# A float32 fast-matrix-product kernel: a changed model for its instruction order, bank halves in the end products, and two subtractions on another engine

## The chip, the cores and the metric

The kernel runs on one core of a Trainium2 chip. A core has four compute engines that the profile names PE (TensorE, the matrix unit; its weight loads are listed apart as PEld), DVE (VectorE), ACT (ScalarE) and POOL (GpSimd). SP (SyncE) only issues transfers. Engines have instruction queues of their own and wait for each other through semaphores. TensorE writes into PSUM, an accumulator memory in eight banks, which VectorE and ScalarE read; all else lies in SBUF. The metric is device time in microseconds (us): the median of several executions of the whole kernel.

## The reference

With 1024 rows of `x`, 512 features `f`, 512 outputs `m` and 64 embeddings `e`:

```python
out_lin = x @ lin_w.T + lin_b
xv = jnp.einsum('bf,efm->bem', x, weight)
zp = jnp.einsum('bf,efm->bem', jnp.square(x), jnp.square(weight))
interaction = 0.5 * jnp.sum(jnp.square(xv) - zp, axis=1)
return out_lin + interaction
```

The sum over `e` of `zp` needs no big product: it is the product of the squares of `x` with the sum over `e` of the squares of `weight`, of the size of the linear part. The big work is `xv`, whose squares are summed over `e`.

## The kernel before

**Work.** The product `xv` is cut into 22 groups of output columns, two of 16 and then twenty of 24 columns, each times 64 embeddings. A group's quarters of the weight arrive by DMA. Sums and differences of the quarters are made, partly by GpSimd transfers that add into SBUF (`dma_add`, lines 462 to 466, called by `outer_sum` and `outer_out`). Seven products (`ORDER`) replace the eight of a two-by-two block product. Each is a *tree*: `tree` (line 729) replaces eight smaller products by seven, with matmuls 384 columns wide in the large groups; `wide_tree` (line 818) has 20 matmuls 256 wide, and takes products 1, 5 and 7 of the large groups. Weight-side sums (`t`) are made by GpSimd. Partial results stay in PSUM banks and are copied from bank to bank by ScalarE (`copy`, line 435) or taken out by VectorE with an addend (`tt`, line 421). At the end ScalarE squares the results and VectorE sums them over `e` into `acc`.

**PSUM.** There are four pairs of banks: `b1`, `b3`, `b2_0`, `b2_1`. A pair is one tensor, and there is also one tensor for each bank of it (`b_l`, `b_r` in the profile), which `wide_tree` uses. The planner keeps its dependencies by banks (its atoms have the size of one bank).

**Small products.** `outer_products` (line 587) does one two-by-two block product with seven `big` products (line 521), each of eight matmuls 256 wide over a whole pair of banks. It is called twice: at the start by `lin` for the linear part, and at the end for the squares' product. In it one pair is copied to another two times, `copy(pair(u2), pair("b1"))` at line 591 and `copy(pair(u3), pair(u2))` at line 599. `big` takes a list of parts `(k, j0, j1)`; as a rule the parts are `(0, 0, 4)` and `(1, 0, 4)`: first weight half 0 over all four cells (both banks), then half 1. The last product alone, at line 603, has four parts that finish the left bank first. Its closing function `leave(0, 1, u2)` reads the pair in two halves at the end of the kernel.

**The end.** While the last trees still run, VectorE adds the summed squares to the linear part in `add_acc` (the instructions at L1043), and the left sides of the squares' product, `xs[3]`, `xs[5]`, `xs[6]`, `xs[7]`, are made of squared blocks of `x`. A `tt` without PSUM operands goes to GpSimd; `minus_both` (line 573; its instruction is L576 in the profile) is one VectorE instruction that gives minus a minus b.

**The order of the work.** All operations are first entered in a `Plan`. `Plan.order` (line 183) then runs its own model of the engines, with a cost for each operation, a fixed `HOP` between an operation's end and its reader's start, a slower rate where VectorE and GpSimd are both at work in SBUF, and one queue for adding transfers. Each engine takes among the ready operations the one with the earliest `latest`, a due time worked out backwards from TensorE's fixed sequence of matmuls and then shifted by an offset from the table `AHEAD_OF` (eighths of a microsecond in base 36, one entry for each position in a part of the program; all even groups share one part, all odd groups another). TensorE takes the ready operation with the lowest key. The order in which the model starts operations is the order in which the program is emitted; each engine's queue is therefore fixed when the kernel is built.

Of the kernel before, what the change touches and what calls it, by code (L numbers as in the profile page):

```python
# [41 lines left out]
0:-1d 1:28mt 2:1rdw 3:28qb 4:28sp 5:1rhs 6:1r1z 7:1o2z 8:r13 9:1ny7 a:3m5 b:1qhi c:1nqc d:1okx e:1qxc f:m62  # L42
g:m61 h:3it i:3jq j:16r0 k:t l:4 m:-k n:v o:2m p:1v q:2s r:1 s:-1 t:o u:-e v:14 w:n x:i y:4 z:k 10:e 11:203
12:1d 13:-1e 14:-8 15:12 16:29 17:v 18:c 19:1m 1a:g 1b:-1g 1c:-5 1d:-2 1e:4oo 1f:-i 1g:-9 1h:k 1i:8 1j:18
1k:-1a 1l:1 1m:-k 1n:19 1o:9 1p:-5 1q:1m 1r:-q 1s:b 1t:-o 1u:1o 1v:4 1w:1d 1x:-1d 1y:-5 1z:j 20:2 21:-1 22:h
23:-j 24:-g 25:3 26:-6 27:w 28:-b 29:-f 2a:x 2b:b 2c:-t 2e:31 2f:-5 2g:1 2h:-a 2i:-7 2j:-u 2k:j 2l:1 2m:r
2n:-v 2o:x 2p:9 2q:3 2r:e 2s:r 2t:-b 2u:-5 2v:p 2w:5 2x:a 2y:a 2z:-l 30:-1 31:-n 32:-3 33:-e 34:i 35:2h 36:s
37:-g 38:-f 39:12 3a:8 3b:z 3c:y 3d:-f 3e:7 3f:-k 3g:h 3h:o 3i:-o 3j:cp 3k:14 3l:1d 3m:x 3n:n 3o:5 3p:-3 3q:-k
3r:k 3s:e 3t:-5 3u:-u 3v:dc 3w:-7 3x:-14 3y:9 3z:23 40:7 41:7 42:c 43:-2 44:-19 45:q 46:-f 47:-3 48:-5 49:-4
4a:-8 4b:-1a 4c:j 4d:-q 4e:2a 4f:3 4g:-3 4h:d 4i:b 4j:s 4k:g 4l:5 4m:6 4n:-16 4o:-c 4p:7 4q:4 4r:-i 4s:q 4t:-b  # L50
4u:-1t 4v:-11 4w:1v 4x:-4 4y:e1 4z:-f 50:-m4 51:-h 52:m 53:p 54:-c 55:12 56:-5 57:-p 58:a 59:-14 5a:-1 5b:-a
5c:-14 5d:-q 5e:-10 5f:-j 5g:-1a 5h:c 5i:2j 5j:g 5k:-18 5l:-1v 5m:fa 5n:-1 5o:k 5p:p 5q:-h 5r:1a 5s:-1r 5t:16
5u:1p 5v:3 5w:q 5x:m 5y:-5 5z:-h 60:r 61:w 62:9 63:-6 64:-1 65:m 66:s 67:x 68:o 69:-2 6a:-17 6b:d 6c:z 6d:-e
6e:-u 6f:-19 6g:f 6h:e 6i:-j 6j:-6 6k:-16 6l:-8 6m:7 6n:-7 6o:-23 6p:-l 6q:-25 6r:t 6s:1z 6t:u 6u:-k 6v:-1
6w:8 6x:-h 6y:2 6z:-14 70:-9 71:-t 72:13 73:1l 74:12 75:h 76:-2p 77:-g 78:i 79:a 7a:-6 7b:16 7c:19 7d:19 7e:r
7f:1b 7g:17 7h:-w 7i:-j 7j:-28 7k:-1m 7l:f 7m:16 7n:9 7o:-w 7p:l 7q:c 7r:-j 7s:-m 7t:2a 7u:5 7v:-k 7w:-5 7x:7
7y:-e 7z:1j 80:9 81:3 82:-8 83:-13 84:-21 85:-1h 86:16 87:-7 88:-14 89:-6 8a:-b 8b:-1e 8c:-1s 8d:2l 8e:o 8f:-7
8g:-t 8h:-e 8i:10 8j:14 8k:r 8l:d 8m:-m 8n:5 8o:-v 8p:18 8q:-g 8r:-v 8s:-6 8t:12 8u:w 8v:12 8w:1y 8x:1n 8y:b
8z:b 90:5 91:18 92:-19 93:-8 94:-h 95:7 96:5 97:f7 98:w 9a:19 9b:-u 9c:-a 9d:9 9e:-b 9f:6 9g:p 9h:-n 9i:-9
9j:6 9k:18 9l:-8 9m:-1 9n:1m 9o:1w 9p:14 9q:11 9r:t 9s:g 9t:-p 9u:u 9v:5 9w:-3 9x:-m 9y:-16 9z:-n a0:-q a1:25  # L60
a2:1k a3:-1l a4:1j a5:7 a6:-2 a7:-1l a8:11 a9:-n aa:dg ab:t ac:-1f ad:-1 ae:-8 af:l ag:-1f ah:1n ai:-6 aj:15
ak:2k al:6 am:y an:3 ao:-1m ap:b aq:-z ar:2 as:p at:3 au:-1 av:-1 aw:-1t ax:g ay:26 az:-t b0:9e b1:u b2:7
b3:-1t b4:-k b5:31 b6:-1p b7:18 b8:t b9:1c ba:8 bb:1y bc:-1n bd:-w be:-3 bf:15 bg:q bh:n bi:-j bj:-6 bk:g bl:i
bm:h bn:8 bo:2 bp:6 bq:-d br:21 bs:-x bt:a bu:-4 bv:1 bw:-t bx:-2 by:-d bz:j c0:-10 c1:-q c2:1d c3:-g c4:-16
c5:22 c6:-1k c7:-2n c8:-15 c9:d ca:-1k cb:6 cc:7 cd:r ce:-t cf:7 cg:-m ch:i ci:-t cj:5 ck:-2d cl:-o cm:-13
cn:-k co:-k cp:p cq:d cr:27 cs:-t ct:-v cu:-1 cv:-1 cw:6 cx:-7 cy:a cz:-3 d0:-1k d1:-1 d2:d d3:9 d4:-s d5:u
d6:16 d7:-4 d8:f d9:-18 da:1a db:-19 dc:-2t dd:-d de:k df:12 dg:c dh:-1y di:-1a dj:3 dk:q dl:-12 dm:-7 dn:-r
do:g dp:-11 dq:-i dr:19 ds:-2g dt:z du:-2e dv:g dw:-e dx:14 dy:v dz:-3z e0:x e1:17 e2:-d e3:-6 e4:l e5:-7
e6:-d e7:n e8:-22 e9:-t ea:5 eb:-q ec:10 ed:l ee:3 ef:9 eg:a eh:1a ei:f ej:-p ek:-v el:3 em:-s en:1s eo:23
ep:6 eq:-28 er:s es:c et:z eu:13 ev:-u ew:5 ex:-1q ey:s ez:-i f0:-7 f1:q f2:-a f3:l f4:-u f5:l f6:f f7:3 f8:d  # L70
f9:-t fa:17 fb:1 fc:-u fd:-i fe:-2 ff:-a fg:j fh:2 fi:-b fj:-2 fk:i fl:1e fm:g fn:-4 fo:1j fp:r fq:-s fr:-16
fs:-27 ft:7 fu:-1c fv:-3 fw:1s fx:i fy:i fz:a g0:4 g1:-15 g2:u g3:-2q g4:32 g5:6 g6:-3c g7:-s g8:-1 g9:-1c
ga:j gb:-2 gc:-1g gd:-2 ge:-s gf:-u gg:1g gh:1i gi:-6 gj:-1e gk:-6 gl:x gm:-i gn:r go:-u gp:-i gq:9 gr:-a gs:3
gt:-b gu:-7 gv:15 gw:-d gx:-1 gy:29 gz:-6 h0:-z h1:1d h2:v h3:-3 h4:7 h5:-j h6:1x h7:-e h8:-6 h9:-u ha:7 hb:2
hc:-w hd:c he:-3 hf:d hg:h hh:-10 hi:19 hj:-b hk:14 hl:-j hm:-5 hn:-1a ho:t hp:b hq:-18 hr:-s hs:-2x ht:-n
hu:b hv:-y hw:-w hx:-1 hy:-1x hz:1d i0:r i1:1 i2:-p i3:-z i5:c i6:1t i7:-s i8:-13 i9:1r ia:-j ib:-6 ic:-2r
id:2 ie:n if:3 ig:p ih:1l ii:l ij:1e ik:5 il:a im:-11 in:-1k io:6 ip:-o iq:-1w ir:17 is:16 it:8 iu:y iv:-11
iw:-b ix:-d iy:x iz:1p j0:-b j1:-c j2:l j4:-7 j5:-c j6:-e j7:8 j8:l j9:b ja:a jb:1 jc:m jd:-h je:p jf:-h jg:-3
jh:-j ji:7 jj:7 jk:2 jl:t jm:-c jn:-a jo:1l jp:-2 jq:m jr:-i js:y jt:-r ju:-l jv:-k jw:18 jx:-r jy:-2 jz:n
k0:11 k1:1q k2:-j k3:-h k4:a k5:-g k6:7 k7:8 k8:1 k9:3 ka:b kb:-3 kc:-a kd:-2 ke:-f kf:-y kg:-n kh:-11 ki:-6  # L80
kj:8 kk:-4 kl:-1a km:z kn:6 ko:-4 kp:f kq:-8 kr:-6 ks:-u kt:-1h ku:-gc kv:-18 kw:-m kx:-16 ky:1 kz:-3o l0:-2b
l1:-1o l2:-1f l3:q l4:e l5:v l6:-1e l7:-27 l8:-14 l9:10 la:h lb:-9 lc:16 ld:o le:2 lf:-n lg:-5 lh:d li:-i
lj:-f lk:-a ll:z lm:10 ln:-v lo:4 lp:6 lq:17 lr:1j ls:-q lt:-1b lu:k lv:h lw:-1c lx:6 ly:t lz:-n m0:-1p m1:1x
m2:-1b m3:-16 m4:-1 m5:1c m6:-z m7:-21 m8:-9 m9:-1w ma:y mb:-1r mc:-p md:-3 me:e mf:-c mg:c mh:1 mi:-5 mj:w
mk:14 ml:o mm:-9 mn:7 mo:-2 mp:-1 mq:-11 mr:-j ms:s mt:-2 mu:-r mv:45 mw:-11 mx:-1b my:-1a mz:q n0:r n1:i
# [12 lines left out]
tb:1t tc:n td:7 te:-3 tf:-u tg:7 th:1j ti:-1m tj:3 tk:-x tl:19 tm:-t tn:e to:-k tp:-a tq:s tr:-2b tt:-6 tu:-5
tv:o tw:1b tx:s ty:j tz:i u0:a u1:1e u2:-u u3:i u4:-6 u5:-j u6:8 u7:2 u8:9 u9:-q ua:1d ub:-1 uc:-r ud:2 ue:-8
uf:-2l ug:-1 uh:w ui:-6 uj:22 uk:-p ul:5 um:-r un:1t uo:-1h up:-5 uq:-8 ur:-7 us:-1b ut:-1a uu:-7 uv:p uw:8  # L100
ux:-a uy:14 uz:18 v0:-m v1:r v2:-20 v3:-o v4:-c v5:-9 v6:-1g v7:10 v8:-2g v9:t va:1d vc:-4 vd:16 ve:-24 vf:-1g
vg:18 vh:-2 vi:-18 vj:-2 vk:-5 vl:-h vm:-3 vn:-s vo:v vp:s vq:d vr:j vs:3 vt:n vu:8 vv:-g vw:d vx:-2y vy:v
vz:s w0:7 w1:-r w2:-2g w3:-2b w4:-17 w5:-12 w6:h w7:f w8:-r w9:-13 wa:-10 wb:-10 wc:-12 wd:k we:-g wf:-4 wg:h
# [32 lines left out]
AHEAD = 20.0  # L136
# [3 lines left out]

def groups(n_m):
    return [16, 16] + [24] * ((n_m - 32) // 24)


class Plan:
    HOP = 0.18

    def __init__(self):
        self.ops = []
        self.writer = {}  # L150
        self.readers = defaultdict(list)
        self.signs = {}
# [30 lines left out]
    def order(self, spare=SPARE):  # L183
# [9 lines left out]
        t = 0.0  # L193
# [953 lines left out]
```

## Time and profile before

| what | us |
|---|---|
| median of 3 runs | 1430.7 |
| lowest and highest run | 1427.57, 1431.08 |
| the profiled execution | 1431.2 |
| its span, first to last instruction | 1429.4 |

All rows of profiles below come from this one profiled execution; its granted TensorE clock was 0.998 of full speed. In the page's first part each engine has its busy time, its share of the span and its count of instructions. In the view of windows a row gives a stretch, and for each engine the busy time and (x) the instructions begun in it. In the chain of waits a row gives the start, the length and what the end of the program hung on at that time; "issue" is time in which an engine waited for nothing that the profile shows. A row of the waits view tells who waited, on whom (after `<-`), the total in us, how often, and the longest. In the timeline a row has the start, the time, engine, line, operation, tiles, shape and count; in brackets the idle time of that engine before it and what ended it. L472 is the matmul of the trees, L529 that of `big`, L429 is `tt`, L439 and L438 the plain and the negative `copy`, L455 the sum over `e`, L464 the adding transfer.

### The profile page before, as it was taken

The page shows a single profiled execution, that of the slowest core. Times are in us where ns is not written, and L with a number is a line of the kernel's source. Part 1 is how long each engine was busy: PE and PEld are TensorE (multiplying, and loading weights), DVE is VectorE, ACT ScalarE, POOL GpSimd, SP SyncE. Part 2 cuts the span into 40 slices and gives each one's busy share as a digit, 9 for nine tenths or more (in the row PEclk, how much of TensorE's full clock was granted, in tenths as well). Part 3 has the DMA queues.
Part 4 walks back from the last instruction along what each step waited for, and adds up shares of the span by engine and source line. Part 5 has one row for each costly group of instructions (what it writes and reads, how often), then busy time and mean ns, then how long its engine had stood idle before and what let it go on. Part 6 is the DMA issues. An engine that isn't in the chain of part 4 may idle for free.

```text
span 1429.4 us, 16910 instructions
## 1 busy us (share of the span) xinstructions
PE 1406.8 (98%) x5264; PEld 986.0 (69%) x5264; DVE 1118.2 (78%) x1462; ACT 810.8 (57%) x1301; POOL 1178.4 (82%) x1121
## 2 busy tenths in 40 slices
PE   9999999999999999999999999999999999999988
PEld 6777766767676666767666676766667676766756
DVE  6577787788869777786878778787878878797896
ACT  3356465566646565564756556464655656565632
POOL 6999888797888879788887979787887978788870
PEclk9999999999999999999999999999999999999999
DMA  8689497686949677794967779496767959686672
GB/s 250 170 189 236 119 207 182 152 200 152 232 117 212 169 166 182 153 234 124 220 163 161 186 154 232 113 227 151 176 169 166 219 122 222 166 185 153 159 175 81
DMA packets 98537, 251.79 MB, mean 176 GB/s; under 512 B 29520, under 2 KB 39248, under 8 KB 98448
## 3 DMA queue, kind: packets, MB, share of 16 engines
q0 software_dynamic: 26448, 134.49, 48.9%
q1 hardware_dynamic: 70848, 115.17, 24.1%
q10 hardware_dynamic: 1152, 1.05, 0.2%
q8 instruction: 43, 0.70, 0.2%
q14 instruction: 46, 0.38, 0.1%
HBM read 127.04 MB, written 6.19 MB: 93 GB/s over the span
## 4 chain that ended last, share of the span: by engine, by line
PE 78%; DMA 8%; POOL 6%; DVE 4%; issue 3%; ACT 1%; SPq 0%; DVEq 0%; POOLq 0%; ACTq 0%
PE b L472 44%; PE b_r L472 16%; PE b_l L472 16%; POOL t L429 4%; DMA ob<-od 2%; DMA oc<-od 2%; PE b L529 2%; DMA w<-T 1%; DVE acc L455 1%; POOL X L429 1%; DVE oa L429 1%; DMA oa<-xT 0%; DMA T<-weight 0%; DVE ob L429 0%; DMA w<-weight 0%
## 5 line engine op out<-in xcount | busy, mean ns | idle before, releaser
L472 PE MATMUL b<-t,X 128*128 128x384 f32 (+1 forms) x1504 | 516.2, 473 | 2.2 <-POOL t L429 1.1
L472 PEld LDWEIGHTS b<-t,X 128*128 128x128 f32 x1504 | 280.2, 190 | 160.1 <-issue 9.2
L429 POOL TENSOR_TENSOR t<-w 128x768 f32<-128x768 f32 (+1 forms) x88 | 162.0, 1841 | 104.3 <-issue 77.3
L429 POOL TENSOR_TENSOR t<-t,w 128x256 f32<-128x256 f32 (+1 forms) x200 | 230.3, 1243 | 10.8 <-PE b L472 6.9
L446 ACT ACTIVATE oa<-oa 128x768 f32<-128x768 f32 (+1 forms) x176 | 144.8, 824 | 122.7 <-DVE oa L429 111.1
L472 PE MATMUL b<-w,X 128*128 128x384 f32 (+1 forms) x576 | 193.9, 469 | 0.3 <-ACT p L439 0.3
L472 PE MATMUL b_l<-t,X 128*128 128x256 f32 x720 | 188.1, 383 | 0.0
L472 PE MATMUL b_r<-t,X 128*128 128x256 f32 x600 | 169.6, 386 | 3.8 <-ACT oa L438 1.1
L455 DVE TENSOR_REDUCE w_sum<-wsq 128x12 f32<-128x768 f32 (+1 forms) x176 | 158.6, 919 | 4.1 <-ACT wsq L446 3.8
L455 DVE TENSOR_REDUCE acc<-oa 128x12 f32<-128x768 f32 (+1 forms) x176 | 160.3, 919 | 1.0 <-ACT oa L446 0.7
L472 PEld LDWEIGHTS b_l<-t,X 128*128 128x128 f32 x720 | 134.2, 190 | 30.9 <-ACT b_l L439 6.8
L472 PEld LDWEIGHTS b_r<-t,X 128*128 128x128 f32 x600 | 109.8, 190 | 59.1 <-issue 9.0
L472 PEld LDWEIGHTS b<-w,X 128*128 128x128 f32 x576 | 108.9, 190 | 58.9 <-ACT p L439 1.4
L446 ACT ACTIVATE wsq<-w 128x768 f32<-128x768 f32 (+1 forms) x132 | 107.0, 822 | 40.6 <-DMA w<-weight 30.6
L429 DVE TENSOR_TENSOR oa<-b,oa 128x768 f32<-128x768 f32 (+1 forms) x88 | 82.1, 932 | 56.9 <-PE b L472 56.5
L439 ACT COPY b<-b 128x768 f32<-128x768 f32 (+2 forms) x98 | 75.7, 772 | 56.5 <-PE b L472 33.3
L472 PE MATMUL b_r<-w,X 128*128 128x256 f32 x400 | 100.0, 381 | 0.9 <-ACT b_r L438 0.6
L429 POOL TENSOR_TENSOR t<-w,t 128x384 f32<-128x384 f32 (+1 forms) x96 | 96.8, 1008 | 2.0
L446 ACT ACTIVATE ob<-ob 128x768 f32<-128x768 f32 (+1 forms) x88 | 72.5, 825 | 36.9 <-DVE ob L429 26.2
L472 PE MATMUL b<-T,X 128*128 128x384 f32 (+1 forms) x264 | 92.9, 481 | 0.5 <-ACT p L439 0.4
L446 ACT ACTIVATE oc<-oc 128x768 f32<-128x768 f32 (+1 forms) x88 | 68.9, 819 | 39.2 <-DMA oc<-od 39.1
L472 PEld LDWEIGHTS b_r<-w,X 128*128 128x128 f32 x400 | 75.3, 190 | 15.4 <-ACT b_r L438 2.5
(157 smaller groups left out, 2712.6 us busy)
## 6 DMA issues: line engine op xcount, KB each, us to landing
w<-weight SPq DMA_DIRECT2D x120, 384.0 KB, 5.2
ob<-od POOLq DMA_DIRECT2D x40, 768.0 KB, 8.5
oc<-od POOLq DMA_DIRECT2D x40, 768.0 KB, 11.6
T<-weight SPq DMA_DIRECT2D x40, 384.0 KB, 3.7
w<-T POOLq DMA_DIRECT2D x20, 768.0 KB, 6.2
T1a<-weight SPq DMA_DIRECT2D x20, 384.0 KB, 3.2
w22a<-weight SPq DMA_DIRECT2D x20, 384.0 KB, 7.6
T1a<-weight POOLq DMA_DIRECT2D x10, 768.0 KB, 14.2
```

The costliest lines, as they stand in the source:

```text
L429: return f(o.ap, a.ap, b.ap)
L439: return nc.scalar.copy(o.ap, i.ap)
L446: lambda _: nc.scalar.activation(o.ap, i.ap, AF.Square), i.atoms, o.atoms)
L455: nc.vector.tensor_reduce(o, x, axis=AX.X, op=ALU.add)
L472: nc.tensor.matmul(a.ap, b.ap, w.ap, start=start, stop=True, skip_group_check=True)
L529: nc.tensor.matmul(a.ap, b.ap, w(k).ap, start=first and k == 0 and j % 2 == 0, stop=True, skip_group_check=True)
```

## The change

Five things are changed. In the planner, `HOP` is 0.19 in place of 0.18, and an operation on a bank starts only when no operation of another engine (TensorE's left out) is still using that bank. An adding transfer is entered with 2.8 us in place of 2.5 per 1024 columns, and starts 0.35 us after it is ready. The table `AHEAD_OF` is a new one: 1685 entries in place of 1665; of the 1701 positions that either table names, 15 have the same offset in both. In `outer_products`, four of the seven products take the four parts that the last one had, and the two copies of a pair become copies of its halves. In the squares' product, `xs[6]` and `xs[3]` become plain subtractions (so GpSimd's), and the signs of `xs[5]`, of the sums `zsum` and of the closing additions follow from that.

```diff
-    HOP = 0.18
+    HOP = 0.19
...
-        def ready(o):
-            return max([0.0] + [d.end for d in o.waits]) + self.HOP
+        def ready(o, e):
+            locked = [x.end for at, _, _ in o.banks for f, x in using.get(at, {}).items() if f != e]
+            return max([0.0] + [d.end for d in o.waits] + locked) + self.HOP + o.lag
...
                     o.end = free[e] + o.land
+                    if e != PE:
+                        for at, _, _ in o.banks:
+                            using.setdefault(at, {})[e] = o
...
-        plan.add({POOL: 0.7}, emit, reads + writes, writes, land=1.8, queue=2.5 * rows / 1024)
+        plan.add({POOL: 0.7}, emit, reads + writes, writes, land=1.8, queue=2.8 * rows / 1024, lag=0.35)
...
-        big("b1", xs[1], ws[1], True, base_key)
-        copy(pair(u2), pair("b1"))
-        big("b1", xs[2], ws[2], False, base_key + 1)
+        halves = ((0, 0, 2), (1, 0, 2), (0, 2, 4), (1, 2, 4))
+
+        def copy_pair(o, i):
+            for k in range(2):
+                copy(reg(o, k * N, N), reg(i, k * N, N))
+
+        big("b1", xs[1], ws[1], True, base_key, halves)
+        copy_pair(u2, "b1")
+        big("b1", xs[2], ws[2], False, base_key + 1, halves)
...
-        big(u2, xs[6], ws[6], False, base_key + 4)
-        copy(pair(u3), pair(u2))
-        big(u3, xs[7], ws[7], False, base_key + 5)
+        big(u2, xs[6], ws[6], False, base_key + 4, halves)
+        copy_pair(u3, u2)
+        big(u3, xs[7], ws[7], False, base_key + 5, halves)
...
-    tt(xs[5], xs[4], x2[1, 0], True)
-    minus_both(xs[6], xs[5], xs[1])
+    tt(xs[5], xs[4], x2[1, 0])
+    tt(xs[6], xs[5], xs[1], True)
     tt(xs[7], xs[1], x2[1, 0], True)
-    minus_both(xs[3], xs[2], xs[6])
+    tt(xs[3], xs[2], xs[6], True)
...
-    tt(two(zsum[1]), w2(0, 1), w2(0, 0))
-    tt(two(zsum[2]), w2(1, 1), two(zsum[1]))
-    tt(two(zsum[4]), w2(1, 0), two(zsum[2]))
-    tt(two(zsum[7]), w2(0, 1), w2(1, 1))
+    tt(two(zsum[1]), w2(0, 1), w2(0, 0), True)
+    tt(two(zsum[2]), w2(1, 1), two(zsum[1]), True)
+    tt(two(zsum[4]), two(zsum[2]), w2(1, 0), True)
+    tt(two(zsum[7]), w2(1, 1), w2(0, 1), True)
...
-            tt(rest[1, 0], rest[1, 0], pair(b), True)
+            tt(rest[1, 0], rest[1, 0], pair(b))
         else:
-            tt(rest[1, 1], rest[1, 1], pair(b))
-            tt(rest[0, 1], rest[0, 1], pair(b))
+            tt(rest[1, 1], rest[1, 1], pair(b), True)
+            tt(rest[0, 1], rest[0, 1], pair(b), True)
...
-            tt(o, o, reg(b, k * 2 * N // n, 2 * N // n), c == 0)
+            tt(o, o, reg(b, k * 2 * N // n, 2 * N // n), True)
```

More of the change, by code (lines that the diff above doesn't have):

```diff
@@ L47 @@
[L47 to L61, printed above, removed]
@@ new lines @@
+bu:1t bv:b bw:o bx:x by:7 bz:-19 c0:-13 c1:v c2:-m c3:b c4:i c5:8 c6:-s c7:x c8:-19 c9:f ca:-v cb:-g cc:s
+cd:-t ce:-1z cf:1r cg:-24 ch:-2o ci:-13 cj:1 ck:-t cl:e cm:-2 cn:1 co:-3a cp:11 cq:-2i cr:w cs:-2a ct:17
+cu:-2e cv:-1a cw:-1q cx:-k cy:9 cz:3y d0:-1 d1:2m d2:-14 d3:-1w d4:-r d5:-1 d6:13 d7:-c d8:7 d9:-d da:-1i
+db:-g dc:-e dd:3 de:-1m df:j dg:27 dh:-c di:1b dj:-1l dk:w dl:-x dm:-w dn:-1 do:v dp:10 dq:b dr:-1n ds:-v
+dt:-s du:1a dv:-7 dw:-13 dx:-b dy:r dz:-n e0:v e1:y e2:-26 e3:o e4:-2d e5:-1o e6:p e7:1y e8:p e9:-1au ea:-2v
@@ new lines @@
+r9:-1o ra:c rb:m rc:-m rd:-a re:-1i rf:-27 rg:-g rh:-e ri:o rj:6 rk:-14 rl:-l rm:-7 rn:1e ro:-1p rp:-h rq:p
+rr:1a rs:-f rt:-9 ru:-7 rv:o rw:2p rx:-1m ry:10 rz:-4 s0:t s1:10 s2:-2k s3:1b s4:-16 s5:12 s6:-2 s7:-c s8:-q
+s9:1t sa:-5 sb:m sc:-1p sd:-1m se:-17 sf:2s sg:-1a sh:-5 si:-39 sj:t sk:-13 sl:-w sm:-3 sn:-2g so:-1b sp:3
+sq:-j sr:17 ss:8 st:-8 su:2e sv:2 sw:v sx:-2b sy:-21 sz:9 t0:2 t1:6 t2:-8 t3:-i t4:-6 t5:1h t6:-20 t7:1n
+t8:-1h t9:10 ta:-9 tb:1h tc:d td:-10 te:-j tf:-f tg:-l th:-2 ti:-1y tj:8 tk:-h tl:1o tm:w tn:6 to:-f tp:-o
@@ new lines @@
+118:-1f 119:-1k 11a:1d 11b:-25 11c:1b 11d:k 11e:-10 11f:r 11h:-10 11i:4 11j:o 11k:-h 11l:1g 11m:7 11n:-q
+11o:-l 11p:-v 11q:-o 11r:-12 11s:1b 11t:-1u 11u:-28 11v:8 11w:a 11x:-2n 11y:-18 11z:-1 120:-5 121:1p 122:-1d
+123:u 124:-6 125:-q 126:o 127:-v 128:-o 129:-z 12a:q 12b:1 12c:n 12d:-u 12e:-8 12f:-2q 12g:4 12h:f 12i:-u
+12j:10 12k:1j 12l:-16 12m:l 12n:7 12o:-5 12p:1c 12q:2n 12r:-l 12s:-b 12t:-24 12u:-r 12v:1y 12w:-m 12x:d 12y:5
+12z:-17 130:e 131:-d 132:10 133:f 134:-o 135:8 136:-1b 137:u 139:h 13a:9 13b:2 13c:1a 13d:-l 13e:-7 13f:-4
@@ new lines @@
+15p:-1y 15q:-r7 15r:-13 15s:-12 15t:p 15u:-o 15v:-5h 15w:-15 15x:p 15y:-1s 15z:c 160:q 161:14 162:-3 163:b
+164:e 165:1j 166:-1q 167:-1b 168:q 169:20 16a:f 16b:-1g 16c:-3 16d:-24 16e:-17 16f:1l 16g:1w 16h:p 16i:5q
+16j:17 16k:-2x 16m:-v 16n:-15 16o:-17 16p:h 16q:15 16r:-b 16s:5 16t:-1o 16u:1c 16v:17 16w:j 16x:w 16y:17
+16z:-1f 170:-l 171:-p 172:-z 173:-21 174:g 175:-1v 176:-2f 177:t 178:-w 179:-7 17a:n 17b:-9 17c:2g 17d:1p
+17e:-6 17f:3y 17g:-o 17h:11 17i:-1c 17j:g 17k:e 17l:l 17m:-2g 17n:1b 17o:-h 17p:b 17q:1f 17r:-1e 17s:-1p
@@ L158, in add @@
     def add(self, costs, emit, reads=(), writes=(), key=None, land=0.0, both=False,
-            banks=(), queue=0.0):
+            banks=(), queue=0.0, lag=0.0):
         op = SimpleNamespace(
             n=len(self.ops), costs=costs, emit=emit, key=key, land=land,
-            deps=set(), succ=[], latest=None, end=None, both=both, banks=banks, queue=queue,
+            deps=set(), succ=[], latest=None, end=None, both=both, banks=banks, queue=queue, lag=lag,
         )
@@ L216, in order @@
         times = [self.HOP]
-        done, late, adding = [], 0.0, 0.0
+        done, late, adding, using = [], 0.0, 0.0, {}
         def release(o):
@@ L239, in pick @@
                 able = [n for n in pending[e]
-                        if ops[n].due < now - late + AHEAD and ready(ops[n]) <= now + 1e-6]
+                        if ops[n].due < now - late + AHEAD and ready(ops[n], e) <= now + 1e-6]
                 return ops[min(able, key=lambda n: (ops[n].key, n))] if able else None
@@ L243, in pick @@
                 return None
-            at = {n: ready(ops[n]) for n in pending[e]}
+            at = {n: ready(ops[n], e) for n in pending[e]}
             for n in sorted((n for n in at if at[n] <= now + 1e-6),
@@ L597, in outer_products @@
         ready(1, m5)
[L598 to L600 removed]
+        big(u2, xs[6], ws[6], False, base_key + 4, halves)
+        copy_pair(u3, u2)
+        big(u3, xs[7], ws[7], False, base_key + 5, halves)
         leave(1, 0, u3)
         leave(1, 1, u3)
[L603 removed]
+        big(u2, xs[3], ws[3], False, base_key + 6, halves)
         leave(0, 1, u2)
```

155 lines of the change are left out of this document (76 added, 79 removed).

## The prediction

> **What bounds the kernel now.** I read the page first, then four long stretches of the windows view, then what TensorE's weight loads wait for, then the chain that ended last.
>
> ```profile
> span 1429.4 us, 16910 instructions
> PE 1406.8 (98%) x5264; PEld 986.0 (69%) x5264; DVE 1118.2 (78%) x1462; ACT 810.8 (57%) x1301; POOL 1178.4 (82%) x1121
> ```
>
> TensorE is busy for 98% of the span, but the ends of matmuls are modelled, so this share hides small stalls. A better measure is how many records fit into a stretch. One row of the chain gives the step of a 384-wide record, one that of a 256-wide record:
>
> ```profile
> 931.35 14.19 PE b L472 x44
> 1350.07 1.73 PE b_l L472 x8
> 150.00:450.00 300.00, 299.64 (x1107) 206.98 (x1106) 237.84 (x314) 177.20 (x285) 253.84 (x236) 1.00 0.74 177
> 450.00:750.00 300.00, 299.70 (x1107) 207.07 (x1106) 237.06 (x315) 176.50 (x284) 249.59 (x233) 1.00 0.74 177
> 750.00:1050.00 300.00, 298.98 (x1101) 205.34 (x1100) 237.27 (x313) 178.54 (x288) 250.21 (x232) 1.00 0.73 172
> 1050.00:1350.00 300.00, 298.97 (x1103) 206.30 (x1102) 239.54 (x315) 182.95 (x290) 254.36 (x235) 1.00 0.75 177
> 1375.00:1400.00 25.00, 20.27 (x65) 12.81 (x64) 24.67 (x21) 7.33 (x10) 14.77 (x13) 0.93 0.84 186
> ```
>
> 14.19/44 is 0.3225 us, 1.73/8 is 0.216 us. A group of 24 columns has four small trees of 14 matmuls 384 wide and three wide trees of 20 matmuls 256 wide; a float32 matmul leaves two records. That is 112 x 0.3225 + 120 x 0.216 = 62.0 us for 232 records, 0.2674 us each. From 150 to 1350 us there are 1107 + 1107 + 1101 + 1103 = 4418 records, 1181.5 us of work in 1200. So **18.5 us** is all that any reordering can find in the middle, though 1197.3 us of it count as busy.
>
> From 1375 to 1400 us the picture turns: VectorE is busy 24.67 of 25 us, and TensorE has only 65 records. There VectorE is the bound, as the chain of waits says too:
>
> ```profile
> 1365.84 0.45 DVE X L576
> 1366.29 2.88 issue
> ...
> 1382.10 3.20 DVE X L1043
> 1385.30 3.42 issue
> 1388.72 0.94 DVE acc L455
> 1389.65 1.13 DVE T1b L576
> 1390.79 1.72 DVE acc L455 x2
> 1392.51 0.88 DVE ob L429
> ```
>
> The two L576 instructions are exactly the two `minus_both` of the squares' product. Both stand on the chain that sets the end. The reader should see the order: the second one, of `T1b`, and three reductions run ahead of the addition into `ob`, and only that addition frees the bank for TensorE. The timeline gives the price:
>
> ```profile
> 1382.10 6.69 DVE L1043 SCALAR_TENSOR_TENSOR X<-T,X 128x928 f32<-128x928 f32 x1
> 1382.26 2.02 POOL L429 TENSOR_TENSOR oa<-oa,oc 128x768 f32<-128x768 f32 x1
> 1385.25 2.55 POOL L429 TENSOR_TENSOR X<-w22a,X 128x1024 f32<-128x1024 f32 x1
> 1393.43 3.45 PE L529 MATMUL b<-w_sum,w22a 128*128 128x256 f32 x8 [4.61 <-DVE ob L429]
> 1395.65 0.84 POOL L464 DMA_DIRECT2D oc<-od  x1 [7.03 <-DVE oa L429]
> 1395.89 1.11 DVE L1043 SCALAR_TENSOR_TENSOR w<-w,w 128x928 f32<-128x928 f32 x1
> ```
>
> The same instruction of 928 elements takes 1.11 us when GpSimd is quiet and 6.69 us beside a run of GpSimd sums.
>
> **The change part by part.**
>
> *Squares' product.* The two L576 instructions become GpSimd subtractions of 1024 elements, 2.55 us each by the row of `X<-w22a,X`. What they take off the chain: 1.13 us for `T1b`, fully, since TensorE waits 4.61 us behind it. For `X` at 1365.84 it is 0.45 + 2.88 = 3.33 us of VectorE, but TensorE was idle little at that place; the first row below shows 0.58 us there. After that, VectorE also waits for transfers of its own. So this one is worth between 0.6 and 3.33 us; I take the middle, 2.1, as no row shows how much of VectorE's lead lasts to 1393. Term: **-3.2 us** (ends -4.6, the whole wait, and +1.9, worked out under the second rival). On GpSimd the two are hidden if they fall into its idle 7.03 us before 1395.65, or after it. The other edits here (a sum for a difference, swapped operands of `zsum`, the signs in `ready` and `leave`) keep engine, size and count: zero.
>
> *Bank halves.* Each `outer_products` now runs four products of a bank pair as left bank, right bank, and copies each bank by itself, so that the next product could start on the left bank while the right one is copied. Stalls at these copies now, and the last product, which is in halves already:
>
> ```profile
> 1370.26 1.99 PE L472 MATMUL b_r<-w,X 128*128 128x256 f32 x8 [0.58 <-ACT b_r L438]
> 12.60 1.99 PE L529 MATMUL b<-ob,oa 128*128 128x256 f32 x8 [1.09 <-ACT b L439]
> 28.46 3.72 PE L529 MATMUL b<-w22b,X 128*128 128x256 f32 x16 [0.22 <-ACT b L439]
> 1416.18 3.69 PE L529 MATMUL b<-w,X 128*128 128x256 f32 x16 [1.18 <-issue]
> 1419.71 2.75 PE L529 MATMUL b<-w_sum,T1b 128*128 128x256 f32 x12
> 1422.50 2.60 DVE L429 TENSOR_TENSOR X<-X,b 128x512 f32<-128x512 f32 x3 [1.31 <-PE b L529]
> 1423.24 1.13 PE L529 MATMUL b<-w_sum,T1b 128*128 128x256 f32 x4 [0.78 <-DVE X L429]
> ```
>
> A record lasts 0.38 us (2.75 less eleven steps of 0.216) but the next can begin after 0.216, so a stall costs the idle time shown plus 0.16. The three stalls are 1.09 + 0.22 + 1.18 + 0.48 = 3.0 us, the most that halves can return.
>
> The last three rows speak against it. The left bank is complete after 8 of the 16 records, at about 1421.6 (1419.71 + 7 x 0.216 + 0.38); VectorE reads it only at 1422.50, after 12, and the last 4 records, which write the right bank, wait until VectorE has read the left one. **The pair is guarded as one thing, not by banks.** If copies are treated alike, each copied half stops TensorE once (0.78 + 0.16 = 0.94 us): the copy waits for the part that has started meanwhile, and the next part waits for the copy. Four pair copies, two halves each: 8 x 0.94 = 7.5 us, less the 3.0 removed, +4.5. Ends: -3.0 and +4.5. The nearest row is the stall, so I take half of the eight, the others lying beside transfers that TensorE waits for at the start: 3.8 - 3.0 = **+0.8 us**. ScalarE gets four more instructions, at 57% busy: nothing.
>
> The Trainium skill, page "PSUM — Partial Sum Buffer", section "PSUM bank collisions raise a hardware error", tells one to guard PSUM with semaphores by bank. By banks the term would be -3.0 and the sum 1421.6; the trace shows a wait by pairs, and I go by the trace.
>
> *The planner's model and its offsets.* `order()` writes out the order of everything by modelled times. Now it lets two engines read a bank one after the other, lengthens an adding transfer from 2.5 to 2.8 us per 1024 columns plus 0.35 us ahead of it, and nearly all offsets in `AHEAD_OF` are new. No instruction is added or dropped in the middle; only places change. Does the trace have such waits between readers?
>
> ```profile
> DVE oc L429 <- ACT p L439: 10.4, 20, 0.7
> DVE od L429 <- ACT od L439: 8.4, 19, 0.7
> PEld b L472 <- ACT p L439: 12.4, 35, 0.8
> PEld b_l L472 <- ACT b_l L439: 10.2, 39, 0.4
> PEld b L472 <- issue: 9.2, 28, 0.6
> PEld b_r L472 <- issue: 9.0, 23, 1.1
> PEld b L472 <- POOL t L429: 7.1, 13, 1.1
> PEld b L472 <- DVE oa L429: 6.8, 23, 0.7
> PEld b_r L472 <- POOL t L429: 6.5, 16, 1.3
> ```
>
> Yes. In a wide tree ScalarE copies bank S to `p`, and VectorE takes the same bank into `oc`; neither writes it, yet VectorE waits 20 times, 10.4 us in all. The old model starts both at once. Those waits are not on TensorE's path themselves, but a late ScalarE copy is: of the 61.2 us in the seven weight-load rows, 22.6 (37%) end with a ScalarE copy. 37% of 18.5 us is 6.8 us, all that this part could give. I take half, **-3.4 us**, since ends of 0.3 us here are partly the plain length of copy and signal. The other end: GpSimd's `t` sums end 13.6 of 61.2 us, 22% or 4.1 us. Planned as longer, the adding transfers fall due earlier and can be issued ahead of these sums on GpSimd's queue, which TensorE then waits for; were those waits doubled, +4.1 us.
>
> *Sum*, on the profiled execution's own 1431.2 us (span 1429.4 and 1.8 around it; the median of the runs is 1430.7, 0.5 less): 1431.2 - 3.2 + 0.8 - 3.4 = **1425.4 us**.
>
> **The rivals.**
>
> *Slower: bank pairs stop TensorE eight times.* Place: both `outer_products`. Price +4.5 us; 1431.2 + 4.5 = 1435.7 us. For it speaks the wait at 1423.24; against it, that at the start other products can lie between. It makes the kernel slower from the point where the other two parts return less than 0.2 us together.
>
> *No difference: GpSimd's run takes the place of the removed work.* The 6.69 us row shows VectorE held until the run of sums was through. Two more sums of 2.55 us in that run hold the next `add_acc` 5.1 us longer, and the term becomes -3.2 + 5.1 = +1.9. Sum: 1431.2 + 1.9 + 0.8 - 3.4 = 1430.5 us. Against it speaks GpSimd's idle 7.03 us at hand.
>
> The Trainium skill, page "SBUF — State Buffer", section "Who interferes with whom", says that of a GpSimd instruction and a VectorE instruction with two SBUF inputs, the one that issues first holds the shared port for its whole length. VectorE began at 1382.10, before GpSimd's 1382.26, and yet lost to the whole run; a start in the trace may only mean that it began to ask. By that rule the removed instructions cost about 1.1 us each, the term is -1.7 (1.13 + 0.58), and the sum is 1426.9.
>
> *By banks after all:* 1421.6 us, if the late wait at 1423.24 has another cause.
>
> *The model doesn't do what it says:* if new offsets trade one wait for another, the middle gives nothing: 1428.8 us; with `t` doubled, 1432.9.
>
> **How the numbers follow.** The forecast and its neighbours 0.42, by banks after all 0.12: faster 0.54. GpSimd in the way 0.13, a middle that gives nothing 0.10, the port rule 0.04: no difference 0.27, as all three times lie there. Eight stalls 0.12, doubled `t` waits beside some of those stalls 0.07: slower 0.19. A measurement of this kernel tells about 0.3% from no change, that is 1426.4 to 1435.0. Lowest: -4.6 - 3.0 - 6.8 gives 1416.8; as the middle could also lose its `t` waits, I go to 1414. Highest: +4.5 and +4.1 with VectorE's term at -3.2 is 1436.6; 1437.
>
> **What would show it.** Right: no two-input subtraction on VectorE at L576 late in the trace; TensorE's wait for `ob` near 1393 under 2 us; over 4430 records between 150 and 1350 us; VectorE's waits for ScalarE on `p` and `od` under half. Right on pairs: gaps near 0.8 us between parts of one product in the first 35 and last 30 us, ended by ScalarE. Wrong: those gaps absent, an `add_acc` of over 8 us, or larger `POOL t` rows.

## The result and the profile after

| | us | ratio to before, 95% interval |
|---|---|---|
| before, median of 4 | 1430.9 (1427.6 to 1431.5) | |
| changed kernel, median of 4 | 1419.4 (1418.7 to 1420.3) | 0.9925 [0.9908, 0.9942] |
| profiled executions | 1431.2 before, 1420.3 after | |

The kernel is 0.75% faster. Forecast was 1425.4 us; the measured time lies inside the range of 1414 to 1437, at twice the forecast gain. Here are the page's totals and the same stretches of the windows view as before:

```profile
span 1418.5 us, 16907 instructions
PE 1398.9 (99%) x5264; PEld 985.7 (69%) x5264; DVE 1113.1 (78%) x1460; ACT 804.1 (57%) x1305; POOL 1184.2 (83%) x1123
150.00:450.00 300.00, 299.97 (x1113) 207.59 (x1112) 240.17 (x315) 176.15 (x285) 257.71 (x243) 1.00 0.75 180
450.00:750.00 300.00, 299.74 (x1112) 207.79 (x1111) 240.00 (x316) 175.86 (x286) 254.38 (x235) 1.00 0.74 179
750.00:1050.00 300.00, 300.00 (x1122) 209.50 (x1121) 242.04 (x317) 176.96 (x290) 252.78 (x234) 1.00 0.73 175
1050.00:1350.00 300.00, 298.93 (x1107) 206.86 (x1106) 242.03 (x317) 182.13 (x292) 255.02 (x234) 1.00 0.74 175
```

In these rows of 1200 us TensorE now has 4454 records in place of 4418. The 36 more are worth 36 x 0.2674 = 9.6 us. (A row counts every record at work in its stretch, so one that spans a boundary is counted twice. By their starts there are 4447 and 4412.) TensorE's busy time over them is 1198.6 us, before it was 1197.3: the busy column shows almost nothing of this gain, the counts show it.

As both kernels issue the same 5264 records in nearly the same sequence, a second account needs no windows. I take the time between the starts of records 0, 700, 5000 and 5263 from the trace, less 0.216 us for each 256-wide record, 0.3225 for each 384-wide and 0.853 for each 512-wide one. What is left is **time lost**, by stage, in us:

| kernel | start | middle | end | median time |
|---|---|---|---|---|
| before | 10.9 | 20.1 | 10.9 | 1430.9 |
| changed | 10.7 | 11.4 | 9.2 | 1419.4 |

Of 10.7 us less, 8.7 come from the middle, 1.7 from the end and 0.2 from the start. The middle has no new instruction; it has another order.

The time lost in the middle consists of small late starts. In the kernel before, 84 records begin 0.1 to 0.2 us late, 9.3 us in all, most of them at the same places of every second group; in the changed kernel 6 do, 0.7 us in all. I put each late start down to the last wait that ended at a weight load in the 0.45 us before it, by what ended that wait. The sums are in us, over records that begin at least 0.01 us late; two of the kernels are described under the experiments:

| what ended the wait | before | the two small edits alone | changed | changed, model without lock |
|---|---|---|---|---|
| a copy by ScalarE | 7.8 | 7.9 | 0.6 | 1.5 |
| a sum `t` by GpSimd | 6.0 | 4.2 | 2.3 | 2.3 |
| VectorE | 1.2 | 1.4 | 6.0 | 8.7 |
| nothing that the profile shows | 5.2 | 5.1 | 2.8 | 1.8 |
| all, with 0.2 for a transfer in the first two | 20.4 | 18.8 | 11.7 | 14.3 |

So late copies and late sums are what the new order took away, and late work of VectorE took back a part.

Next, who stops TensorE now. These rows of the waits view are of the matmuls themselves:

```profile
PE b L536 <- ACT b L446: 4.9, 7, 0.7
PE b L536 <- DVE ob L436: 3.0, 1, 3.0
```

And some of the places in the timeline, the first three of the start, the others of the end:

```profile
12.44 1.13 PE L536 MATMUL b<-ob,oa 128*128 128x256 f32 x4 [0.66 <-ACT b L446]
14.28 1.13 PE L536 MATMUL b<-ob,oa 128*128 128x256 f32 x4 [0.71 <-ACT b L446]
...
31.48 2.86 PE L536 MATMUL b<-w22b,X 128*128 128x256 f32 x12 [0.71 <-ACT b L446]
...
1380.96 1.26 PE L536 MATMUL b<-w_sum,w22a 128*128 128x256 f32 x4 [3.00 <-DVE ob L436]
...
1403.59 1.13 PE L536 MATMUL b<-T1a,X 128*128 128x256 f32 x4 [0.70 <-ACT b L446]
...
1406.30 2.86 PE L536 MATMUL b<-w,X 128*128 128x256 f32 x12 [0.71 <-ACT b L446]
...
1412.53 1.13 PE L536 MATMUL b<-w_sum,T1b 128*128 128x256 f32 x4 [0.78 <-DVE X L436]
```

The wait for `ob` costs more than its 3.0 us. In the trace the granted TensorE clock is 0.50 from 1381.83 to 1385.24 us, just behind it, and 1.00 around that stretch. The same four records take 2.76 us in it and 1.45 us after it:

```profile
1382.02 2.76 PE L479 MATMUL b<-t,X 128*128 128x384 f32 x4
...
1386.64 1.45 PE L479 MATMUL b<-t,X 128*128 128x384 f32 x4
```

The kernel before has such a stretch too, from 1393.00 to 1396.42 us. The eight records at 1393.43, which the prediction shows at 3.45 us, take 1.89 us at 1398.01. Half of 3.41 us, about 1.7 us, is my estimate of the price of one stretch in which TensorE is at work throughout, worked out from the 0.50 and the 3.41 us.

The copied halves stop TensorE seven times, 0.66 to 0.71 us each; of the eight that the prediction named as possible, one lies beside other work. The 3.0 us wait for `ob` was 4.6 before. Its chain is one of VectorE and GpSimd again:

```profile
1369.49 1.63 POOL L436 TENSOR_TENSOR t<-w,t 128x384 f32<-128x384 f32 x1
1369.84 4.67 DVE L1056 SCALAR_TENSOR_TENSOR X<-X,X 128x1024 f32<-128x1024 f32 x1
1370.46 2.96 POOL L436 TENSOR_TENSOR X<-X,w22a 128x1024 f32<-128x1024 f32 x1
1375.31 1.21 DVE L1056 SCALAR_TENSOR_TENSOR X<-X,X 128x1024 f32<-128x1024 f32 x1
1375.46 2.72 POOL L436 TENSOR_TENSOR oa<-oa,oc 128x768 f32<-128x768 f32 x1 [2.04 <-DVE oa L436]
```

The third row is one of the two subtractions that moved to GpSimd. It follows a sum whose row begins before that of VectorE's `add_acc`, and the `add_acc` takes 4.67 us; five microseconds later, where GpSimd was idle, the same kind of instruction takes 1.21.

### The profile page after: what moved, and what is told of

The parts are those of the page before. It is cut to its first block, busy times and chain, and to the rows that moved or that the text cites. A ratio compares the mean times of both kernels' runs of the same rounds, so it can differ in the third digit from the quotient of the medians.

```text
span 1418.5 us, 16907 instructions
## 1 busy us (share of the span) xinstructions
PE 1398.9 (99%) x5264; PEld 985.7 (69%) x5264; DVE 1113.1 (78%) x1460; ACT 804.1 (57%) x1305; POOL 1184.2 (83%) x1123
## 4 chain that ended last, share of the span: by engine, by line
PE 91%; DMA 4%; POOL 1%; DVE 1%; issue 1%; ACT 1%; SPq 0%; ACTq 0%; POOLq 0%; DVEq 0%
PE b L479 52%; PE b_r L479 18%; PE b_l L479 18%; PE b L536 3%; DMA w<-weight 2%; POOL t L436 1%; DMA ob<-od 1%; DMA ob<-lin_wT 0%; DMA oa<-xT 0%; POOL X L436 0%; DMA w<-T 0%; DVE ob L436 0%; DVE oa L436 0%; DVE X L436 0%; ACT wsq L453 0%
## 5 line engine op out<-in xcount | busy, mean ns | idle before, releaser
L479 PEld LDWEIGHTS b<-t,X 128*128 128x128 f32 x1504 | 276.0, 190 | 166.8 <-DVE oa L436 20.4
L436 POOL TENSOR_TENSOR t<-t,w 128x256 f32<-128x256 f32 (+1 forms) x200 | 242.3, 1299 | 4.1
L446 ACT COPY b<-b 128x768 f32<-128x768 f32 (+1 forms) x102 | 76.5, 750 | 60.8 <-PE b L479 38.8
L446 ACT COPY p<-b 128x768 f32<-128x768 f32 (+1 forms) x76 | 57.2, 753 | 56.2 <-PE b L479 56.1
L436 POOL TENSOR_TENSOR oc<-ob,p 128x512 f32<-128x512 f32 (+1 forms) x80 | 85.1, 1120 | 4.5 <-ACT p L446 4.5
```

Source lines behind the costliest of these rows:

```text
L436: return f(o.ap, a.ap, b.ap)
L446: return nc.scalar.copy(o.ap, i.ap)
L479: nc.tensor.matmul(a.ap, b.ap, w.ap, start=start, stop=True, skip_group_check=True)
```

## The experiments

Each kernel computes the whole result. Medians are given with the ratio to the kernel before that ran on the same chip, and its interval. The median of that kernel lies between 1430.9 and 1432.0 us in these comparisons, so 1 us between the medians of two experiments can be the chip's.

**Halves on tensors of one bank.** The split products, their copies and their readers use one tensor for each bank; a reader of a pair becomes two of a bank.

```diff
-            outs = [reg(o, j * C, C) for j in range(j0, j1)]
+            outs = [bank(o, j // 2, j % 2 * C, C) if len(parts) == 4 else reg(o, j * C, C)
+                    for j in range(j0, j1)]
...
-                copy(reg(o, k * N, N), reg(i, k * N, N))
+                copy(bank(o, k), bank(i, k))
...
-            tt(o, o, reg(b, k * 2 * N // n, 2 * N // n), True)
+            for j in range(2 // n):
+                plan.count -= j
+                p = Reg(o.tile, o.off + j * N, N)
+                tt(p, p, bank(b, k if n == 2 else j), True)
```

> The changed kernel with the four split products, their copies and their readers on tensors of one bank each instead of a pair. Theory (a pair of banks is guarded as one thing, and each copied half stops TensorE for about 0.7 us of idle time): the seven idle times of 0.66 to 0.72 us ended by ScalarE's copies in the two small products, and the 0.78 us near the end, go or fall under 0.2 us; the time falls by 4 to 6 us from 1419.4, to 1413.5 to 1415.5 us. Rival (the copies are late for another reason, the stalls stay): 1419.4 us within 1 us.

Measured 1415.7 us, 0.9894 [0.9874, 0.9915], with one run of four at 1421.2. At the end no stall is left between the parts of the products; this timeline is of that run:

```profile
1398.75 1.89 PE L537 MATMUL b_l<-T1a,X 128*128 128x256 f32 x8
1400.48 1.89 PE L537 MATMUL b_r<-T1a,X 128*128 128x256 f32 x8
1402.21 1.89 PE L537 MATMUL b_l<-w,X 128*128 128x256 f32 x8
1403.93 1.89 PE L537 MATMUL b_r<-w,X 128*128 128x256 f32 x8
1405.66 1.89 PE L537 MATMUL b_l<-w_sum,T1b 128*128 128x256 f32 x8
1407.39 1.89 PE L537 MATMUL b_r<-w_sum,T1b 128*128 128x256 f32 x8
```

Every row starts 1.73 us after the one before it, eight records of 0.216. Time lost at the end falls from 9.2 to 5.2 us. At the start it stays (10.7 and 10.5): in this run TensorE waits there 2.1 us for VectorE and 1.5 us for a load instead, and its granted clock is 0.50 from 22.48 to 25.89 us. The theory holds; its amount was put a little too high, since the start has other waits behind the stalls.

**Whole pairs again.** Two parts and one copy in place of four and two, with the offsets of all other operations in their places.

```diff
-            for k in range(2):
-                copy(reg(o, k * N, N), reg(i, k * N, N))
+            copy(pair(o), pair(i))
+            plan.skip()
...
-        big("b1", xs[1], ws[1], True, base_key, halves)
+        big("b1", xs[1], ws[1], True, base_key, both)
+        plan.skip()
+        plan.skip()
```

> The changed kernel with the four products and the two copies over whole pairs again, all other offsets of the table kept in their places. Theory (halves on a pair cost more than they save): seven stalls of about 0.87 us go, three or four longer ones of 1.1 to 1.3 us come back; at the start part of that is hidden by transfers: 1416.5 to 1419 us. Rival (halves pay as they were meant): 1421 to 1422.5 us.

Measured 1431.9 us, 0.9998 [0.9987, 1.001]. The theory misses by 13 us and its rival by 9. The time lost at the start is 22.6 us, and 14.3 of it fall between records 400 and 700, behind the edited product; the middle, 11.8, is like that of the changed kernel, and the end, 7.7, is better. The planner had put other work in another order there; TensorE's waits from 90 to 155 us are those of tree matmuls:

```profile
PE b L483 <- ACT p L450: 3.8, 1, 3.8
PE b L483 <- DVE ob L440: 3.5, 2, 3.2
```

The granted clock is 0.50 for 10.2 us between 127.3 and 147.8 us, and TensorE is at work in 9.5 of them: by the same estimate 4.7 us more. With these waits that makes some 12 of the 14.3 us.

So this run says nothing of halves. Taking one part out moves the planner's whole order, and the same doubt hangs over every run that plans anew, the one with single banks too. The next run keeps the order.

**Whole pairs in the frozen order.** The order of emission is that of the changed kernel; only the matmuls within the four products change places, and the pair is copied after the fourth part.

```diff
+            if len(parts) == 4 and key not in (-1000 + 6, 1e6 + 6):
+                at, first_cell = n // 2, 2 * (n % 2)
...
             for k in range(2):
                 copy(reg(o, k * N, N), reg(i, k * N, N))
+                plan.ops[-1].emit = None
+            last.then = (lambda: nc.scalar.copy(pair(o).ap, pair(i).ap),
+                         plan.ops[-2].banks + plan.ops[-1].banks)
```

> The changed kernel, its order of emission kept, but the four split products as first weight half over both banks, then the second, and one copy of the whole pair after each instead of two halves. Theory (halves on a pair bring about nothing): seven stalls of 0.87 us go, four of 1.1 to 1.3 us come, 1418 to 1420.5 us; the 12 us that the undoing cost with a new order don't show. Rival (the halves themselves are worth several us): 1423 us or more.

Measured 1418.8 us, 0.9915 [0.9899, 0.9932], beside 0.9925 for the changed kernel: no difference that can be told. Four stalls of 1.09 to 1.18 us stand where seven of 0.7 were. The wait for `ob` is 3.02 us, but here no slower clock follows it, so the wait alone doesn't decide that; a stretch at 0.50 stands at 22.49 us instead. **Halves on a pair bring nothing**; the 12 us of the run before were the order's.

**The two subtractions on VectorE again.** `minus_both` and the old signs are put back; planned anew.

```diff
-    tt(xs[5], xs[4], x2[1, 0])
-    tt(xs[6], xs[5], xs[1], True)
+    tt(xs[5], xs[4], x2[1, 0], True)
+    minus_both(xs[6], xs[5], xs[1])
     tt(xs[7], xs[1], x2[1, 0], True)
-    tt(xs[3], xs[2], xs[6], True)
+    minus_both(xs[3], xs[2], xs[6])
```

> The changed kernel with the two subtractions of the squares' product on VectorE again, offsets kept. Theory (they stand on VectorE's chain at the end): 1.5 to 4 us slower than the changed kernel, 1421 to 1423.5 us, with TensorE's wait for ob before the first product of the squares growing from 3.0 us. Rival (the end is held by other work on VectorE and GpSimd, so they are hidden): 1419.4 us within 0.7 us.

Measured 1417.2 us, 0.9897 [0.9882, 0.9912]; its slowest run (1418.25) is below the fastest of the changed kernel (1418.73). The theory fell: with the two on VectorE the kernel is faster, not slower. Time lost at the end is 5.3 us in place of 9.2, with no wait for `ob` before the first product and no stretch at 0.50 there. But here too the order is new.

**The same in the frozen order.** Only the engine of the two instructions changes.

```diff
     for op, engine in plan.order():
+        if op.n in moved:
+            engine = DVE
```

> The changed kernel, its order of emission kept as it is, with the two subtractions alone on VectorE at the same places of that order. Theory (on GpSimd they hold the add_acc of 4.67 us and the sum into oa behind it): 1416.5 to 1418.5 us, that add_acc under 3 us. Rival (the gain of the run with both on VectorE came from another order at the end): 1419 us or more.

Measured 1418.3 us, 0.9913 [0.9898, 0.9928]: the median is 1.1 us below the changed kernel's, where the theory puts it, but the intervals overlap. The profile is plainer than the time:

```profile
1369.87 2.38 DVE L1058 SCALAR_TENSOR_TENSOR X<-X,X 128x1024 f32<-128x1024 f32 x1
1372.17 1.21 DVE L436 TENSOR_TENSOR X<-X,w22a 128x1024 f32<-128x1024 f32 x1
1377.03 1.21 DVE L436 TENSOR_TENSOR T1b<-T1a,X 128x1024 f32<-128x1024 f32 x1
1380.02 1.13 PE L536 MATMUL b<-w_sum,w22a 128*128 128x256 f32 x4 [2.03 <-DVE ob L436]
```

The `add_acc` of 4.67 us takes 2.38, both subtractions 1.21 each, and VectorE begins the sum into `oa` behind them 1.13 us earlier (1373.31 for 1374.44). The wait for `ob` falls from 3.00 to 2.03, and the clock behind it stays at 1.00. These two, 1.0 and about 1.7 us, are the 2.7 us that the end loses less in this trace (6.5 for 9.2). So on VectorE the two cost 2.4 us and save 2.3 at one `add_acc` alone. What of the 2.2 us of the run before is order, and what the engine, these two runs don't settle.

**The two small edits alone, on the kernel before.** Halves and GpSimd subtractions with the old model and the old offsets; a half has the offset of the whole it came from.

```diff
+                plan.count -= k
                 copy(reg(o, k * N, N), reg(i, k * N, N))
...
+            plan.count -= len(parts) == 4 and n % 2 and key not in (-1000 + 6, 1e6 + 6)
```

> The kernel before with the halves and the two GpSimd subtractions alone, old model and old table (a half has the offset of the whole it came from). Theory as predicted (-3.2 for the subtractions, +0.8 to +3.1 for the halves): 1428.5 to 1431 us, 1101 to 1107 records in each 300 us of the middle as before. Rival (these two edits bring most of the gain): under 1425 us.

Measured 1438.1 us, 1.0042 [1.0027, 1.0057]: 6.2 us slower than the kernel before on that chip, where the theory forecast a small gain. The middle is little changed (18.4), start (13.6) and end (15.9) are worse. How much of this is the halves' and how much the subtractions' isn't told apart. TensorE's longest waits:

```profile
PE b L472 <- DVE ob L429: 7.7, 1, 7.7
PE b L530 <- ACT b L439: 6.1, 7, 1.9
```

Seven stalls at copies came, and the wait for `ob` grew from 4.6 to 7.7 us, though two instructions left VectorE. The timeline shows why:

```profile
1383.38 1.61 POOL L429 TENSOR_TENSOR t<-w22b,t 128x384 f32<-128x384 f32 x1
1383.62 10.94 DVE L1051 SCALAR_TENSOR_TENSOR X<-X,X 128x1024 f32<-128x1024 f32 x1
1384.35 2.41 POOL L429 TENSOR_TENSOR oa<-oa,oc 128x768 f32<-128x768 f32 x1
1386.12 1.86 POOL L429 TENSOR_TENSOR w<-w_sum 128x512 f32<-128x512 f32 x1
1387.34 2.93 POOL L429 TENSOR_TENSOR X<-w22a,X 128x1024 f32<-128x1024 f32 x1
1389.63 1.46 POOL L464 DMA_DIRECT2D oc<-od  x1
1390.23 3.24 POOL L429 TENSOR_TENSOR T1b<-T1a,X 128x1024 f32<-128x1024 f32 x1
```

The moved subtraction into `T1b` lengthens GpSimd's run, and the `add_acc` of 1024 elements that VectorE began 0.24 us after the first of these sums had begun takes **10.94 us**. It is the second rival of the prediction, in its own place; there an `add_acc` of over 8 us was named as its mark. Around the end of the wait of 7.7 us the granted clock is 0.50 for 6.83 us, twice as long as in the kernel before.

**The model.** Five kernels differ in the planner alone: the changed one with the whole model of before; the one before with the new model; the one before without any offset, in both models; and the changed one without the readers' lock.

```diff
-            locked = [x.end for at, _, _ in o.banks for f, x in using.get(at, {}).items() if f != e]
+            locked = []
```

That one line is the last of the five; the old model has also 2.5 us and no 0.35 us for the adding transfer, and `HOP` 0.18.

> The changed kernel built with the old model (no lock between readers of a bank, adding transfer 2.5 us without the 0.35 us ahead, hop 0.18), new table and all other edits kept. Theory (the model's knowledge of readers and transfers finds the middle's order): the middle loses most of its gain, 1110 records or fewer in each 300 us between 150 and 1350 us, 1425 us or more. Rival (the new offsets alone do it): 1419 to 1422 us.

> The kernel before with the new model alone; old table, old small products. Theory (the model is what finds the better order): 1422 to 1427 us. Rival (offsets belong to the model they were searched with; the model alone does nothing or harm): 1430 us or more.

> The kernel before with no offsets at all (empty table), old model. It says what the offsets are worth: slower than before, by 10 to 60 us. To be compared with zero_new: if the model by itself orders better, zero_old is slower than zero_new by 3 us or more; if not, they are within 3 us or the other way round.

> The kernel before with no offsets at all, new model. Theory (model better by itself): at least 3 us faster than zero_old. Rival (gain is in the offsets): within 3 us of zero_old, or slower.

> The changed kernel built with a model without the lock between readers of a bank, but with the longer adding transfer and the new hop; new table. Theory (the readers' lock is what the new offsets rest on): the middle loses 20 us or more as with the whole old model, 1440 us or more. Rival (the transfers are): 1419 to 1428 us.

| offsets | model | median, us | ratio to before | lost in the middle |
|---|---|---|---|---|
| old | old (before) | 1430.9 | | 20.1 |
| old | new | 1481.7 | 1.0347 [1.0317, 1.0377] | 69.1 |
| none | old | 1478.0 | 1.0321 [1.0257, 1.0385] | 58.1 |
| none | new | 1476.1 | 1.0308 [1.027, 1.0345] | 60.7 |
| new | old | 1453.0 | 1.0146 [1.0114, 1.0178] | 37.8 |
| new | new without lock | 1418.2 | 0.9912 [0.9892, 0.9932] | 13.9 |
| new | new (changed) | 1419.4 | 0.9925 [0.9908, 0.9942] | 11.4 |

Without offsets the two models can't be told apart: the new one doesn't order better by itself. The old offsets are worth some 47 us under the model that they go with. Under the other model they are worth nothing (1481.7 for 1476.1), and the new ones lose 34 us, more than half. And of the new model's three parts the lock is the one that doesn't matter. Without it ScalarE's and VectorE's instructions change places in the trace, 2.5 us more are lost in the middle and 5.0 less at the end (4.2), and the time is the same. The changes in the transfers and in `HOP` are what the new offsets stand on: the two kernels with the new offsets and no lock, 1453.0 and 1418.2 us, differ in these alone. Which of the two it is isn't told apart here. That theory of mine, that the lock carries the gain, fell.

**Both better forms together.** Tensors of one bank, and the subtractions on VectorE.

> The changed kernel with both: the split products on tensors of one bank each, and the two subtractions of the squares' product on VectorE again. Theory (two separate losses, copies that stop TensorE and a GpSimd run that holds VectorE): they add, 1412.5 to 1414.5 us. Rival (both shorten the same wait at the end): 1415 to 1417 us.

Measured **1412.6 us**, 0.9871 [0.9856, 0.9886], as the theory says, the fastest of all, 6.8 us below the changed kernel. Time lost is 10.3 at the start, 12.1 in the middle and 2.3 at the end. The gains add within the spread: 3.7 and 2.2 alone, 6.8 together.

## Why the prediction was right, and where not

**Where the room was.** The count of records gave 18.5 us in the middle and a VectorE-bound end; that account held. By the stages the room in the middle was 20.1 us; 18.5 is short of it, as records at the boundaries of the rows are counted twice there. The middle now loses 9.6 us less by the windows, 8.7 by the stages.

**The middle, -3.4 forecast, about -9 measured.** This is the term that was mis-sized, and it is nearly all of the difference. I put its end at -6.8, as ScalarE's copies ended 37% of the listed weight-load waits. Record by record that share was right: late starts behind ScalarE's copies made 7.8 of 20.4 us, and 7.2 of them went. The step that failed was to take half of it, and to enter GpSimd's `t` only as a possible loss of 4.1 us, where it gave 3.7 us. VectorE's late work took 4.8 us back. The view's totals alone can't tell this. After the change the same view reads:

```profile
PEld b L479 <- DVE oa L436: 20.4, 59, 1.4
PEld b L479 <- DVE ob L436: 15.1, 44, 0.8
PEld b L479 <- issue: 11.5, 34, 0.5
PEld b_l L479 <- ACT b_l L446: 4.6, 11, 1.2
PEld b L479 <- POOL t L436: 4.4, 10, 0.6
PEld b L479 <- ACT p L446: 3.8, 13, 0.4
```

ScalarE's two rows fell from 22.6 to 8.4 us and `POOL t` on `b` from 7.1 to 4.4, as the gain asks; but VectorE's row on `oa` rose from 6.8 to 20.4, and the middle is faster all the same. In the rows of the timeline a weight load begins 0.2 to 0.3 us before its matmul (1376.18 and 1376.51 in the changed kernel), and a wait there need not reach TensorE: the row on `oa` rose by 13.6 us, the late starts behind all of VectorE's work by 4.8. What the profile could have said was the whole room; how much of it another order takes can't be read from it.

**The reason given for the middle.** It has two halves. That late copies of ScalarE hold TensorE is borne out by the late starts. That the lock between readers takes them away is not: without it VectorE's waits for ScalarE on `p` into `oc` are back (20 times, 10.2 us, as before), and yet the late starts behind copies are 1.5 us and the time is the same. So the direction was right, with half of its reason, and the order that brought it stands on the offsets and on the changes in the transfers and `HOP`.

**The subtractions, -3.2 forecast.** The runs show a loss in place of a gain: +2 us with a new order, about +1 us in the frozen order, which can't be told from zero, both against the changed kernel, and TensorE's wait 3.1 us longer in the order of before. On GpSimd they hold up an `add_acc` on VectorE, the mechanism of the second rival, which put the term at +1.9. The step that failed was to take VectorE's time on the chain as saved, and GpSimd's idle 7.03 us as the place where the work would go. The planner put one of the two beside an `add_acc`, at 1370.46. The end is still 1.7 us better; with the edits alone it was 5.0 us worse (10.9 to 15.9), so that gain belongs to the new order. The prediction also left out the slower clock behind the wait for `ob`, which its row of 3.45 us shows. The two terms of the small edits sum to -2.4 us, and start and end together gave -1.9; that this fits is luck, as the two edits alone cost 6.2 us.

**The rule on the shared port.** The Trainium skill, page "SBUF — State Buffer", section "Who interferes with whom", gives the port to the one that issues first. The prediction took its row at 1382.10 to speak against that, as VectorE began before GpSimd's sum at 1382.26. It overlooked the row before, which ends at 1382.53:

```profile
1380.97 1.56 POOL L429 TENSOR_TENSOR T1b<-w_sum,T1a 128x512 f32<-128x512 f32 x1
```

So GpSimd was first there. In the two rows of this kind above GpSimd's sum is the first by its recorded start as well, at 1369.49 and at 1383.38, but there a transfer's issue on GpSimd ends only after the `add_acc` begins (1370.08 and 1383.97), so which of the two got the port first can't be seen. In all three cases the `add_acc` ends 1.0 to 1.1 us, about its own length, after the last sum of GpSimd's run: 1388.79 after 1387.80, 1374.51 after 1373.42, 1394.56 after 1393.47. Where VectorE began first, at 1375.31, it kept its 1.21 us, and GpSimd's sum at 1375.46 took 2.72 us, for 1.81 of a sum of the same shape at 1385.87. So the trace agrees with the rule where it is clear who began; it also shows that VectorE got no turn between the sums of a run.

**The halves, +0.8 forecast.** The mechanism was right: a pair is guarded as one thing, and the seven stalls of 0.66 to 0.71 us are close to the 0.78 read off the last product. In the frozen order the term is 0.65 us by the medians, which can't be told from zero. That this is near +0.8 is partly luck: seven stalls came where the term has four, and whole pairs cost four stalls in that order where the term has the 3.0 us of before. By single banks I put the halves at -3.0 us. Against whole pairs in the frozen order the run with single banks gives -3.1 (1418.8 to 1415.7), but it was planned anew, so its order may have a share in that. The guard by bank that the Trainium skill's page "PSUM — Partial Sum Buffer" names in its section "PSUM bank collisions raise a hardware error" is what the run with single banks does, without these stalls.

**Signs named ahead.** More than 4430 records in the middle (4454), no subtraction at the old line late in the trace, and gaps near 0.8 us ended by ScalarE came out; the wait for `ob` under 2 us didn't (3.0), nor were VectorE's waits for ScalarE all halved: `oc` on `p` fell from 10.4 to 1.2, but `od` on `p` rose from 1.2 to 5.1, and `od` on `od` fell only from 8.4 to 7.1. Larger `POOL t` rows and an `add_acc` of over 8 us didn't appear.

## What to carry to other kernels

A modelled order and the offsets searched with it are one thing: an edit that touches the plan re-orders work far from itself, so its worth is measured with the order frozen. Count records in a stretch rather than trust a pipelined engine's busy share. And work in halves of a buffer pays only when the halves are also guarded apart.

## What the runs showed of the hardware that was not expected

One two-input instruction of 1024 elements on VectorE took 1.21 us where GpSimd was idle when it began, and 10.94 us, nine times as long, where its row begins 0.24 us after the first sum of a run of GpSimd's and it ends 1.09 us after the last. GpSimd's own subtractions of that size, counted from the end of the row before each, took 2.3 to 2.4 us in the changed kernel and in the run with the two small edits. VectorE bears nearly all of a meeting with a run that is under way.

The granted TensorE clock was 0.50 for 3.41 us behind waits of TensorE of 3.00 and 4.61 us, for 6.83 us at one of 7.73 us, and 1.00 behind one of 2.03 us. Behind one of 3.02 us it was 0.50 in the run with single banks and 1.00 in the frozen run with whole pairs. What decides it these traces don't show.
